# FFN inputs of twelve tiles: transposed by VectorE in 32x32 blocks and a copy through DRAM, in place of TensorE; centring moved to ScalarE

## The chip, the cores and the metric

The kernel runs on one core of a Trainium2 chip. The metric is the device time of one execution in microseconds (us). Three runs of the kernel before took 278.52, 279.04 and 279.18 us; their median is 279.04 us. One further execution was taken by the hardware profiler; every line of a profile shown here is from such an execution.

## The reference, cut to what matters

There are 2048 tokens of 512 features, in float32. Two gated residual steps follow each other:

```python
h = layernorm(x)                         # (x - mean) / sqrt(var + 1e-5), over the features
e = expert of the token's id             # 4 experts, each with one 512x512 matrix C[e]
y = (silu(h @ C[e].T) * (h @ C[e].T)) @ C[e]      # gate, up and down are the same matrix
x = x + tanh(g_xattn) * y
h = layernorm(x)
gates, which = top 2 of softmax(h @ wr.T)         # 8 routes
s = silu(silu(h @ w1.T) @ w3.T) @ w2.T
out = zeros; out[which[:, k]] += gates[:, k] * s  # the 8 rows named by the route's number, over all tokens
x = x + tanh(g_ffn) * out
```

The second step adds only to the first 8 rows of the result, so it is a weighted sum over all tokens; but each token goes through the two 512x512 layers and the routing first.

## The kernel before, in words

Tokens are sorted by expert and cut into 17 tiles ("passes") of 128. Passes 0 to 12 hold one expert each; passes 13 to 16 are mixed: four groups of 32 tokens, each with an expert of its own, so that four expert matrices are loaded for such a pass and its matmuls are 32 columns wide. The passes run in the order 0, 1, 2, 3, 4, 5, 13, 6, 7, 8, 14, 9, 10, 15, 11, 12, 16 (`order`, line 383).

A pass goes through these steps. GpSimd gathers its rows of x (`gather`, line 389). VectorE takes the mean and variance and subtracts the mean (`centre`, lines 340 to 401). TensorE transposes the tile, four 128x128 transposes into one PSUM tile tp_a, and ScalarE copies it to SBUF as hT (`turn_in`, lines 380 and 410). TensorE makes z (`up`, line 453); ScalarE and VectorE make g from it (lines 466 and 467). TensorE transposes g, ScalarE copies it as gT (`turn_mid`, line 473). TensorE makes y (`down`, line 453); VectorE adds it to x (line 481), GpSimd scatters x to the output (line 482). VectorE normalizes the new x (`norms`, lines 340 to 373 and 505), together with the inverse root for a later pass. At last TensorE transposes that (tp_f) and ScalarE copies it into hT2 (`turn_out`, line 515; lines 520 to 527 for the mixed passes, whose groups of 32 go to places known only at run time).

Every engine works through its own instructions in the order in which the code writes them; nothing is rescheduled. The loop (line 876) is a software pipeline. Iteration i issues z of the i-th pass in the order, the input transposes of the next, the centring of the one after, the gather and the matrix load of the third after, y of the pass before, tp_f of the one before that, the norm of the pass before, and the transposes of g. Matrices are loaded in SyncE's DMA queue into seven buffers (`load`, line 443), x into five.

The FFN works on two halves of 1024 tokens, hT2[0] and hT2[1]. Passes 0 to 7 fill the first. When it is complete, `sums_of_hT` issues on TensorE the logits of the router (lg, line 699), and on VectorE four sums T of quarters of hT2 (lines 598 to 602) and the transposes of the logits (lt, line 710): the first of the sums stands ahead of the two lt. Then the first layer follows as fast matrix product of seven products p1 to p7 (X, Y, Z, line 622, with additions on VectorE, line 640), routing, the second layer (v, line 730) and the weighted sum (acc). These are a generator, `ffn`, of which `step()` issues one piece; the loop calls it twice an iteration, before and after `turn_mid`, so that the pieces lie between the passes' own matmuls. logits and X come from one pool of two PSUM buffers (`ps_x`): the first X after the logits takes the buffer of the first lg. At the end of the loop the pieces that remain are issued one after another.

In the iteration in which the first half's logits are issued the second `step()` is left out:

```python
        for b in range(NB):
            if last[b] == i - 2:
                hT_sums[b] = sums_of_hT(b)
                running.append(ffn(b))
        if last[0] != i - 2:
            step()
```

Of the kernel before, what the change touches and what calls it, by code (L numbers as in the profile page):

```python
# [19 lines left out]
P = 128  # L20
# [5 lines left out]
def tile_gated_moe_ffn(  # L26
# [59 lines left out]
    xp = ctx.enter_context(tc.tile_pool(name="xp", bufs=5))  # L86
    work = ctx.enter_context(tc.tile_pool(name="work", bufs=3))
    small = ctx.enter_context(tc.tile_pool(name="small", bufs=4))
    ps_mm = ctx.enter_context(tc.tile_pool(name="ps_mm", bufs=2, space=bass.MemoryType.PSUM))
    ps_x = ctx.enter_context(tc.tile_pool(name="ps_x", bufs=2, space=bass.MemoryType.PSUM))  # L90
    ps_y = ctx.enter_context(tc.tile_pool(name="ps_y", bufs=1, space=bass.MemoryType.PSUM))
# [213 lines left out]
    def row_tables():  # L305

        pad = ct_([P, NP], F32, "pad")
        nc.vector.tensor_scalar(pad, tok, 1.0, float(4 * NT), ALU.is_lt, ALU.mult)
        nc.vector.scalar_tensor_tensor(to_row, tok, -1.0, pad, ALU.add, ALU.add)

        pads = ct_([P, E], F32, "pads")
        nc.vector.tensor_sub(pads, size[:, 2, :], num[:, 0, :])
        behind = ct_([P, E, NU - NF], F32, "behind")
        nc.vector.tensor_tensor(
            behind,
            later[:, E : 2 * E, NF:NU],
            pads.unsqueeze(2).to_broadcast([P, E, NU - NF]),
            ALU.mult,
        )
        psum = ct_([P, NU - NF], F32, "psum")  # L320
        nc.vector.tensor_reduce(psum, behind.rearrange("p e n -> p n e"), AX.X, ALU.add)
        nc.vector.tensor_sub(psum, place0[:, NF:NU], psum)
        nc.vector.tensor_scalar(
            first, psum, float(-(NB - 1) * TB), float(TB), ALU.add, ALU.min
        )


    hT2 = [ct_([P, KC, TB + (Q if b == NB - 1 else 0)], F32, f"hT2_{b}") for b in range(NB)]
    s1 = ct_([P, KC, TB], F32, "s1")
    acc = ps_acc.tile([P, D], F32, tag="acc", name="acc")  # L330
    accT = ps_acc.tile([P, KC, NR], F32, tag="acc", name="accT")
# [10 lines left out]
        nc.vector.bn_aggr(mv, st)  # L342
        return mv

    def inverse_roots(mvs_, names):


        n = range(len(names))

        def new(tag):  # L350
            return [small.tile([P, 1], F32, tag=tag, name=f"{tag}_{name}") for name in names]

        v, r, q, w, rs = new("v"), new("r"), new("q"), new("w"), new("rs")
        for i in n:
            nc.vector.tensor_scalar_add(v[i], mvs_[i][:, 1:2], EPS)
        for i in n:
            nc.vector.tensor_scalar(
                r[i].bitcast(I32), v[i].bitcast(I32), -0.5, float(0x5F3759DF), ALU.mult, ALU.add
            )
        for i in n:  # L360
            nc.vector.scalar_tensor_tensor(q[i], r[i], v[i], r[i], ALU.mult, ALU.mult)
        for i in n:
            nc.vector.tensor_scalar(w[i], q[i], 0.375, -1.25, ALU.mult, ALU.add)
        for i in n:
            nc.vector.tensor_scalar(w[i], w[i], q[i], 1.875, ALU.mult, ALU.add)
        for i in n:
            nc.vector.tensor_mul(r[i], r[i], w[i])
        for i in n:
            nc.vector.scalar_tensor_tensor(q[i], r[i], v[i], r[i], ALU.mult, ALU.mult)
        for i in n:  # L370
            nc.vector.tensor_scalar(q[i], q[i], -0.5, 1.5, ALU.mult, ALU.add)
        for i in n:
            nc.vector.tensor_mul(rs[i], r[i], q[i])
        return rs
# [22 lines left out]
    def centre(p):  # L397

        mvs[p] = moments(xs[p], f"a{p}")
        hs[p] = work.tile([P, D], F32, tag="h", bufs=4, name=f"h_a{p}")  # L400
        nc.vector.tensor_scalar(hs[p], xs[p], mvs[p][:, 0:1], None, ALU.subtract)  # L401

    def scale(*ps):
        for p, rs in zip(ps, inverse_roots([mvs.pop(p) for p in ps], [f"a{p}" for p in ps])):
            rss[p] = rs

    def turn_in(p):
        tp = transposed(hs.pop(p), f"a{p}")
# [83 lines left out]
    def norms(p_in, p_out):  # L492


        if p_out is None:
            return
        xt = x1s.pop(p_out)
        mv = [moments(xt, f"f{p_out}")]
        names = [f"f{p_out}"]
        if p_in is not None:  # L500
            mv.append(mvs.pop(p_in))
            names.append(f"a{p_in}")
        rs = inverse_roots(mv, names)
        h = work.tile([P, D], F32, tag="h", bufs=4, name=f"h_f{p_out}")
        nc.vector.tensor_scalar(h, xt, mv[0][:, 0:1], rs[0], ALU.subtract, ALU.mult)
        hs2[p_out] = h
        if p_in is not None:
            rss[p_in] = rs[-1]

    def turn_out(p):  # L510

        tp = transposed(hs2.pop(p), f"f{p}").rearrange("p (k t) -> p k t", k=KC)
        if p < NF:
            b, t = divmod(p, TB // P)
            nc.scalar.copy(hT2[b][:, :, t * P : (t + 1) * P], tp)  # L515
            return
        for i in range(G):
            n = (p - NF) * G + i
            place = NF * P + n * Q - (NB - 1) * TB
            at = nc.values_load(  # L520
                first[0:1, n : n + 1],
                engines=[ACT],
                min_val=min(place - E * (Q - 1), TB),
                max_val=min(place, TB),
                skip_runtime_bounds_check_because="its place less at most E (Q - 1) pads, at most TB",
            )
            nc.scalar.copy(hT2[NB - 1][:, :, bass.ds(at, Q)], tp[:, :, i * Q : (i + 1) * Q])

    def route(b, lt):

# [60 lines left out]
    def sums_of_hT(b):  # L591


        lgs = [logits(b, half) for half in range(2)]
        b11, b12 = hT2[b][:, 0:2, 0:HB], hT2[b][:, 0:2, HB:TB]
        b21, b22 = hT2[b][:, 2:4, 0:HB], hT2[b][:, 2:4, HB:TB]
        ts = [ffp.tile([P, 2, HB], F32, tag=f"T{i}", name=f"T{i}_{b}") for i in range(1, 5)]
        nc.vector.tensor_sub(ts[0], b12, b11)
        lts[b] = [turned(b, half, lg) for half, lg in enumerate(lgs)]
        nc.vector.tensor_sub(ts[1], b22, ts[0])  # L600
        nc.vector.tensor_sub(ts[2], b22, b12)
        nc.vector.tensor_sub(ts[3], b21, ts[1])
        return b11, b21, b22, ts

    def first_layer(b):
# [14 lines left out]
        def product(out_ps, a, bb, c, start):  # L620
            for k in range(2):
                nc.tensor.matmul(  # L622
                    out_ps,
                    a[:, k, c * P : (c + 1) * P],
                    bb[:, k, :],
                    start=start and k == 0,
                    stop=k == 1,
                    skip_group_check=True,
                )
# [62 lines left out]
    def logits(b, half):  # L692


        lg = ps_x.tile([P, P], F32, tag="x", name=f"lg_{b}_{half}")
        for k in range(KC):
            cols = hT2[b][:, k, half * HB : (half + 1) * HB].rearrange("p (t c) -> p t c", t=TT)
            for i in range(P // Q):
                nc.tensor.matmul(  # L699
                    lg[i * Q : (i + 1) * Q, :],  # L700
                    wr[:, k, :],
                    cols[:, :, i * Q : (i + 1) * Q],
                    start=(k == 0),
                    stop=(k == KC - 1),
                )
        return lg
# [116 lines left out]

    SHORT = 1
    last = {b: max(i for i, p in enumerate(order) if min(p // (TB // P), NB - 1) == b) for b in range(NB)}
    running, hT_sums, lts, w1_sums = [], {}, {}, []

    def step():
        if running:
# [23 lines left out]
    rest = slice(order[1] + 1, NU)  # L853
    nc.gpsimd.tensor_copy(held[0:1, rest], which[0:1, rest])
    first_in(order[0])
    scale(order[0])
    centre(order[1])
    scale(order[1])
    load(order[2])
# [11 lines left out]
    turn_mid(order[1])  # L871
    norms(order[3], order[0])
    load(order[4])
    summing = sums_of_w1()
    owed = []
    for i in range(2, NP + 2):
        if i < NP:
            up(order[i])
        if i + 1 < NP:
            turn_in(order[i + 1])  # L880
        if i + 2 < NP:
            centre(order[i + 2])
        if i + 3 < NP:
            gather(order[i + 3])
            load(order[i + 3])
        if i <= NP:
            down(order[i - 1])
        turn_out(order[i - 2])
        if i <= NP:
            norms(order[i + 2] if i + 2 < NP else None, order[i - 1])  # L890
        step()
        if i > NP:
            step()
        if 5 <= i < 9:
            next(summing)
        if i == 2:
            w1 = load_w(w1T, "w1")
            wr = load_w(wrT, "wr")
        if i == 7:
            w3 = load_w(w3T, "w3")  # L900
            w2 = load_w(w2T, "w2")
        if i < NP:
            turn_mid(order[i])
        for b in range(NB):
            if last[b] == i - 2:
                hT_sums[b] = sums_of_hT(b)
                running.append(ffn(b))
        if last[0] != i - 2:
            step()
    fetched = False  # L910
    while running:
        step()
# [50 lines left out]
```

## Time and profile before

| | before |
|---|---|
| median of three runs | 279.04 us |
| the profiled execution's own time | 277.53 us |
| its span, first to last instruction | 275.8 us |
| TensorE busy | 266.6 us (97%) |
| VectorE busy | 148.7 us (54%) |
| ScalarE busy | 69.3 us (25%) |
| GpSimd busy | 39.3 us (14%) |
| moved by DMA | 42.54 MB, 154 GB/s over the span |
| granted TensorE clock | 1.00 |

The span lies inside the execution's own time; the 1.7 us between them are before the first and after the last instruction. A group of the profile reads: line, engine, operation, output and inputs, shape, number of instructions, then busy microseconds, mean nanoseconds of one, and the idle time of the engine ahead of them with what ended it. A row of a timeline reads: start, duration, engine, line, operation, and in brackets the idle time ahead of it. A chain or timeline merges neighbours of one kind and gives their number. Where a row names as releaser an instruction that had long been done, something else was waited for, often a DMA. PE is TensorE, DVE VectorE, ACT ScalarE, POOL GpSimd; SPq is SyncE's queue.

### The profile page before, as it was taken

What the parts mean: (1) busy time and instruction counts of PE and PEld (TensorE: products, weight loads), DVE (VectorE), ACT (ScalarE), POOL (GpSimd) and SP (SyncE); (2) the same over time, 40 slices, a digit from 0 to 9 for tenths busy, and PEclk for the clock granted to TensorE, in tenths of its full rate; (3) what the DMA queues carried; (4) which work ended last, traced back from release to release, by engine and by line L of the source; (5) the groups of instructions that cost most, each with busy time, mean ns of one, the idle gap of its engine ahead of it and who ended that gap; (6) DMA issues with size and microseconds to landing.
All of it is one profiled execution on the core that took longest, in us unless ns stands there. A gap on an engine that the chain in (4) does not pass through costs nothing.

```text
span 275.8 us, 3562 instructions
## 1 busy us (share of the span) xinstructions
PE 266.6 (97%) x1173; PEld 125.4 (45%) x1173; DVE 148.7 (54%) x593; ACT 69.3 (25%) x134; POOL 39.3 (14%) x63
## 2 busy tenths in 40 slices
PE   5889999999999999999999999999999999999994
PEld 2445455544355454444344444534245444344362
DVE  6677877777888769918263481516253620711000
ACT  2022232232232231223143232312113233311120
POOL 6520122221122211211110010101010000000000
PEclk9999999999999999999999999999999999999999
DMA  0697998545669996697304084001000000000000
GB/s 1 217 354 277 408 402 334 173 155 206 228 225 402 389 409 258 173 398 264 112 26 166 2 312 180 38 0 40 0 12 2 0 0 1 0 0 2 0 0 2
DMA packets 20722, 42.54 MB, mean 154 GB/s; under 512 B 2143, under 2 KB 2207, under 8 KB 20704
## 3 DMA queue, kind: packets, MB, share of 16 engines
q1 hardware_dynamic: 17952, 33.66, 34.0%
q0 software_dynamic: 2720, 8.65, 8.3%
q8 instruction: 9, 0.15, 0.2%
q14 instruction: 9, 0.07, 0.1%
q10 hardware_dynamic: 32, 0.01, 0.0%
HBM read 38.10 MB, written 4.47 MB: 154 GB/s over the span
## 4 chain that ended last, share of the span: by engine, by line
PE 94%; DVE 2%; DMA 2%; issue 1%; ACT 0%; DVEq 0%
PE z L453 22%; PE y L453 21%; PE v L730 20%; PE X L622 10%; PE Y L622 5%; PE tp_f L380 3%; PE tp_a L380 3%; PE tp_g L380 3%; PE Z L622 2%; PE acc L742 1%; PE lg L699 1%; DMA x<-in_x_dram,from_row 1%; DMA idt<-in_ids_dram 1%; PE accT L758 1%; PE o L814 0%
## 5 line engine op out<-in xcount | busy, mean ns | idle before, releaser
L453 PE MATMUL z<-m,hT 128*32 128x512 f32 (+1 forms) x232 | 61.8, 595 | 0.2 <-ACT hT L428 0.2
L453 PE MATMUL y<-m,gT 128*32 128x512 f32 (+1 forms) x232 | 61.4, 594 | 0.0
L730 PE MATMUL v<-w,s 128*128 128x512 f32 (+1 forms) x136 | 57.3, 570 | 0.0
L730 PEld LDWEIGHTS v<-w,s 128*128 128x128 f32 x136 | 25.0, 190 | 27.2 <-issue 26.7
L453 PEld LDWEIGHTS z<-m,hT 128*32 128x32 f32 (+1 forms) x232 | 22.6, 146 | 29.5 <-issue 28.1
L453 PEld LDWEIGHTS y<-m,gT 128*32 128x32 f32 (+1 forms) x232 | 22.6, 146 | 27.8 <-issue 27.8
L482 POOL DMA_INDIRECT out_dram<-x,to_row x17 | 17.2, 1011 | 84.9 <-DVE x L481 82.7
L389 POOL DMA_INDIRECT x<-in_x_dram,from_row x17 | 16.7, 984 | 77.5 <-DVE h_a L401 22.9
L467 DVE SCALAR_TENSOR_TENSOR g<-z,rs_a,g 128x512 f32<-128x512 f32 x17 | 12.7, 750 | 27.1 <-ACT g L466 27.0
L466 ACT ACTIVATE g<-z,rs_a 128x512 f32<-128x512 f32 x17 | 11.7, 687 | 51.3 <-PE z L453 51.3
L481 DVE SCALAR_TENSOR_TENSOR x<-y,tg,x 128x512 f32<-128x512 f32 x17 | 12.7, 749 | 16.9 <-PE y L453 16.8
L738 ACT ACTIVATE s<-v 128x512 f32<-128x512 f32 (+1 forms) x17 | 9.7, 572 | 41.9 <-PE v L730 41.9
L515 ACT COPY hT<-tp_f 128x512 f32<-128x512 f32 x13 | 7.6, 587 | 43.5 <-PE tp_f L380 43.5
L340 DVE BATCH_NORM_STATS2 st_a<-x 128x6 f32<-128x512 f32 x16 | 11.0, 688 | 7.5 <-DMA x<-in_x_dram,from_row 7.5
L622 PE MATMUL X<-T,S 128*128 128x512 f32 x32 | 15.0, 592 | 0.0
L380 PEld LDWEIGHTS tp_f<-ident,h_f 128*128 128x128 f32 x68 | 8.2, 141 | 10.2 <-issue 10.2
L340 DVE BATCH_NORM_STATS2 st_f<-x 128x6 f32<-128x512 f32 x17 | 11.8, 695 | 0.6
L380 PEld LDWEIGHTS tp_a<-ident,h_a 128*128 128x128 f32 x64 | 7.7, 140 | 9.4 <-issue 9.1
L640 DVE TENSOR_TENSOR s<-X,c 128x512 f32<-128x512 f32 x4 | 2.8, 692 | 16.2 <-PE X L622 16.2
L473 ACT COPY gT<-tp_g 128x512 f32<-128x512 f32 x17 | 10.0, 586 | 5.3 <-PE tp_g L380 5.3
L380 PE MATMUL tp_f<-ident,h_f 128*128 128x128 f32 x68 | 10.4, 276 | 0.0
L380 PE MATMUL tp_g<-ident,g 128*128 128x128 f32 x68 | 10.2, 273 | 0.0
(165 smaller groups left out, 271.6 us busy)
## 6 DMA issues: line engine op xcount, KB each, us to landing
m<-in_ctxT_dram SPq DMA_DIRECT2D x29, 1024.0 KB
w<-in_w1T_dram SPq DMA_DIRECT2D x1, 1024.0 KB
w<-in_w3T_dram SPq DMA_DIRECT2D x1, 1024.0 KB
w<-in_w2T_dram SPq DMA_DIRECT2D x1, 1024.0 KB
x<-in_x_dram,from_row POOLq DMA_INDIRECT x17, 6.2
out_dram<-x,to_row POOLq DMA_INDIRECT x17, 6.1
wr<-in_wrT_dram SPq DMA_DIRECT2D x1, 64.0 KB
x_first<-out_dram SPq DMA_DIRECT2D x4, 4.0 KB
```

The lines of the kernel that those rows point to most:

```text
L340: nc.vector.bn_stats(st, xt)
L380: nc.tensor.transpose(tp[:, k * P : (k + 1) * P], h[:, k * P : (k + 1) * P], ident)
L389: nc.gpsimd.indirect_dma_start(out=xt, out_offset=None, in_=x, in_offset=bass.IndirectOffsetOnAxis(ap=from_row[:, p : p + 1], axis=0),)
L453: nc.tensor.matmul(out_ps[i * n : (i + 1) * n, :], lhs[:, k * P + i * n : k * P + (i + 1) * n], m[:, k, :], start=(k == 0), stop=(k == KC ...
L466: nc.scalar.activation(g, z, AF.Silu, scale=rs)
L467: nc.vector.scalar_tensor_tensor(g, z, rs, g, ALU.mult, ALU.mult)
L473: nc.scalar.copy(gT, tp)
L481: nc.vector.scalar_tensor_tensor(xt, y, tg[:, 0:1], xt, ALU.mult, ALU.add)
L482: nc.gpsimd.indirect_dma_start(out=out, out_offset=bass.IndirectOffsetOnAxis(ap=to_row[:, p : p + 1], axis=0), in_=xt, in_offset=None, bou ...
L622: nc.tensor.matmul(out_ps, a[:, k, c * P : (c + 1) * P], bb[:, k, :], start=start and k == 0, stop=k == 1, skip_group_check=True,)
L730: nc.tensor.matmul(v, s1[:, k, c_b + t * P : c_b + (t + 1) * P], w3[:, k, c0 : c0 + n], start=(k == 0), stop=(k == KC - 1),)
L738: nc.scalar.activation(s2, v, AF.Silu)
```

## The change

For the twelve passes 0 to 11 the final transposes leave TensorE and their copies leave ScalarE. VectorE transposes the normalized tile in 32x32 blocks straight into the place of a group of four passes (`set_turned`). Within a block the transpose is then right, but each quarter of the partitions still holds its own 32 tokens of every pass; a copy puts them in place. When a group of four is complete, ScalarE's DMA queue writes it to DRAM (`put`), and one iteration later reads it back in four DMAs, one for each quarter of the partitions (`fetch`). `go_on_turning` issues one of these stages an iteration, behind the centring. The mixed passes and pass 12 keep the old way. hT2 is now four tiles, one for each 512 tokens.

The centring of the passes' inputs becomes an activation on ScalarE, which computes mean minus x; the inverse root takes the other sign to make up for it. Only the first pass is centred on VectorE as before.

The first half's logits are issued two iterations later than before, and `step()` is called in every iteration.

```diff
+    NS = NF // 4 * 4
+    hT2 = [ct_([P, G, KC, P], F32, f"hT2_{b}") for b in range(NB * 2 - 1)]
+    hT2.append(ct_([P, KC, HB + Q], F32, "hT2_last"))
...
         hs[p] = work.tile([P, D], F32, tag="h", bufs=4, name=f"h_a{p}")
-        nc.vector.tensor_scalar(hs[p], xs[p], mvs[p][:, 0:1], None, ALU.subtract)
+        nc.scalar.activation(hs[p], xs[p], AF.Identity, bias=mvs[p][:, 0:1], scale=-1.0)
...
         for i in n:
-            nc.vector.tensor_scalar(q[i], q[i], -0.5, 1.5, ALU.mult, ALU.add)
+            nc.vector.tensor_scalar(q[i], q[i], -0.5 * signs[i], 1.5 * signs[i], ALU.mult, ALU.add)
...
+    def set_turned(p):
+        b, i = divmod(p, 4)
+        place = hT2[b]
+        h = hs2.pop(p)
+        nc.vector.transpose(
+            place.rearrange("p q k (i t) -> p k q i t", i=4)[:, :, :, i, :],
+            h.rearrange("p (k q t) -> p k q t", k=KC, q=4),
+        )
+        if i == 3:
+            copy = dram.tile([P, 4, KC * P], F32, tag=f"copy{b}", name=f"copy_{b}")
+            turning.append(lambda: put(place, copy))
+
+    def put(place, copy):
+        nc.scalar.dma_start(copy, place.rearrange("p q k c -> p q (k c)"))
+        turning.append(lambda: fetch(place, copy))
+
+    def fetch(place, copy):
+        for q in range(4):
+            nc.scalar.dma_start(
+                place[q * Q : (q + 1) * Q].rearrange("f g k c -> f g (k c)"),
+                copy[:, q, :].rearrange("(g f) c -> f g c", g=4),
+            )
+
+    def go_on_turning():
+        if turning:
+            turning.pop(0)()
...
         if i + 2 < NP:
             centre(order[i + 2])
+        go_on_turning()
         if i + 3 < NP:
             gather(order[i + 3])
             load(order[i + 3])
         if i <= NP:
             down(order[i - 1])
-        turn_out(order[i - 2])
+        if order[i - 2] >= NS:
+            turn_out(order[i - 2])
         if i <= NP:
             norms(order[i + 2] if i + 2 < NP else None, order[i - 1])
+            if order[i - 1] < NS:
+                set_turned(order[i - 1])
         step()
...
         for b in range(NB):
-            if last[b] == i - 2:
+            if last[b] + 2 + 2 * (b == 0) == i:
                 hT_sums[b] = sums_of_hT(b)
                 running.append(ffn(b))
-        if last[0] != i - 2:
-            step()
+        step()
```

## The prediction

> **What bounds the kernel now.** I read the page's busy shares first (TensorE 97%, VectorE 54%, ScalarE 25%), then the chain that ended last. From 15.4 us to 271 us that chain is TensorE alone: what leaves TensorE shortens the span, what makes it wait lengthens it. The chain in order of time, where the first half of the FFN starts (start, us, what):
>
> ```profile
> 101.51 0.44 PE tp_f L380 x4
> 101.94 0.44 PE tp_g L380 x4
> 102.38 1.88 PE lg L699 x64
> 104.26 3.63 PE z L453 x8
> 107.89 0.44 PE tp_a L380 x4
> 108.33 3.57 PE y L453 x32
> 111.90 0.59 PE tp_f L380 x4
> 112.49 1.72 PE X L622 x4
> ```
>
> The four transposes of a tile cost 0.44 us; after 32-column matmuls the next group costs 0.15 more, whichever it is. Between the logits lg and the first product X lie 8.2 us of other work. Then the groups, for the durations and for who waits:
>
> ```profile
> L340 DVE BATCH_NORM_STATS2 st_a<-x 128x6 f32<-128x512 f32 x16 | 11.0, 688 | 7.5 <-DMA x<-in_x_dram,from_row 7.5
> L401 DVE TENSOR_SCALAR h_a<-x,mv_a 128x512 f32<-128x512 f32 x16 | 7.8, 486 | 0.6
> L598 DVE TENSOR_TENSOR T<-hT 128x1024 f32<-128x1024 f32 x2 | 2.4, 1220 | 5.3 <-ACT hT L527 5.3
> L710 DVE STREAM_TRANSPOSE lt<-lg 128x128 f32<-128x128 f32 x4 | 1.1, 303 | 2.2 <-PE lg L699 2.2
> ```
>
> VectorE already waits for gathered x tiles, 7.5 us in all. GpSimd's timeline shows why:
>
> ```profile
> 94.17 0.98 POOL L389 DMA_INDIRECT x<-in_x_dram,from_row  x1 [6.14 <-DVE h_a L401]
> 95.45 1.02 POOL L482 DMA_INDIRECT out_dram<-x,to_row  x1 [0.30 <-DVE v_a L355]
> 102.40 0.98 POOL L389 DMA_INDIRECT x<-in_x_dram,from_row  x1 [5.93 <-DVE h_a L401]
> 103.69 1.02 POOL L482 DMA_INDIRECT out_dram<-x,to_row  x1 [0.30 <-DVE v_f L355]
> 110.91 0.98 POOL L389 DMA_INDIRECT x<-in_x_dram,from_row  x1 [6.21 <-DVE T L602]
> ```
>
> Each scatter follows its gather after 1.3 us; the next gather starts 7 us after the scatter. The VectorE instructions named had ended before, so it is the scatter's landing, whose buffer the gather takes over. The loop paces itself: nine rounds from 35.69 to 110.91, 8.36 us each. A TensorE iteration is z 3.44 + y 3.44 + three transposes of 0.44 = 8.2 us: the two are level today.
>
> **What the Trainium skill says.** "VectorE: DVE Perf Modes", The three transpose paths: VectorE transposes in 32x32 blocks only; 311 ns for 128x128, and this trace has 303. "DMA: Bandwidth & Descriptors", Anatomy of one DMA: a DMA's semaphore wait happens on the issuing sequencer, before dispatch. No dependent DMA on ScalarE's queue shows this here. "SBUF — State Buffer", Door 1 (the port swizzle): 32 partitions reach 8 of 16 ports, 189 GB/s measured against 328 for 128. No run here shows it yet. "TensorE: Matmul & The Clock Gate", Part 1: after an idle window of some 3.4 us TensorE runs at half clock until about 3.4 us of work. The trace agrees in kind: the first ten warming matmuls (line 200), after an idle start, took 3.84 us, the next 21 took 4.70, so ten cost 1.6 us too much.
>
> **The change, part by part.**
>
> Removed from TensorE: twelve tiles x 0.44 = **-5.3 us**. Removed from ScalarE: twelve copies of 0.59 (line 515), off the path.
>
> Added to VectorE: twelve block transposes of 128x512. No row has that shape. The nearest, the statistics, also pass 512 elements: 0.69 us. Not below 0.53 (T's 1.22 us for 1024 columns less the 0.69 of line 640's additions for 512: the columns without the start-up), not above four of 303 ns, 1.2 us; I take 0.69. They add 8.3 us and the centring's 7.8 leaves, in iterations where VectorE is busy 5.7 to 6.4 of 8 us: nothing. That cover gone, 0.2 us an iteration.
>
> Added to ScalarE: 16 centrings at 0.63 (nearest: Silu from SBUF to SBUF, line 647, 629 ns; bounds 0.5 and 0.75), and 15 DMA issues at 0.4 (SyncE's take 0.37, ScalarE's two at the end 0.5 each). ScalarE is three quarters idle. But in its queue gT's copy now stands behind the centring, which waits for a gather, and behind the DMAs, which wait for each other. y needs gT 3.9 us after tp_g (z and tp_a lie between): later than that, TensorE waits. The sign moved into the constants costs nothing, the instructions are the same.
>
> DMA: three tiles of 1.05 MB written and read back, 6.3 MB on 42.5. The first pair falls at 58 to 70 us, where the DMA share is 0.52 to 0.58: nothing. The second falls where it is 1.04 and more, 86 to 104 us, and beside the loads after 107. The third has about 30 us from z of the last pass to its logits and needs some 20: nothing. SyncE's queue keeps its order; lane counts of its semaphores now include ScalarE's DMAs, but those it waits for are landed long before.
>
> Moved: the first half's logits go from iteration 10 to iteration 12, and the guard that kept an FFN step from following them is gone. X now stands directly behind lg. X takes the PSUM buffer of lg's first half, so it waits for VectorE's transpose of it (line 710), which stands behind T (line 598), which stands behind the whole norm of that iteration. Before, 8.2 us covered this.
>
> Where is TensorE then, if nothing makes it wait? y(14), of a mixed pass, ended at 111.90; it has eight tp_f (3.5) and lg (1.88) less ahead of it: 106.5. Then tp_g 0.59, z 3.43, tp_a 0.44, y(9) 3.44: 114.4; tp_f(14), tp_g 0.44 each, lg 1.88: X at **117.2**.
>
> When may X start? The gather for that iteration was issued at 110.91. The loop doesn't shorten with TensorE; two small waits for VectorE in it (0.4 us) vanish, longer scatters beside 2 MB more traffic (8.0 to 8.1 us are seen in full stretches, against 6.8) give that back. Awaited gathers landed 5.9 to 7.1 us after issue; 6.9 beside the new copy: 117.8. VectorE then runs statistics 0.69 + 0.18, x 0.75, norm 3.42 (44.24 to 47.66 in its timeline), block transpose 0.69, T 1.22, lt 0.30: **125.1**. The wait is **+7.9 us**. Some of it may fall earlier, before y(9): x of pass 15 lands at 102.40 + 6.7 = 109.1, ScalarE's centring ends at 110.6, four DMA issues at 112.3, gT at 112.9, where y(9) wants it at 111.0. That 1.9 is inside the 7.9, since VectorE is later still.
>
> T also needs the copy back. Out: issued after pass 10's centring, about 102.4; 1.05 MB at half of 405 GB/s (SyncE's loads share) 5.2 us and 2 to land (the first small DMA took 1.74): 109.6. Back: issues end at 112.3; 5.2 us at half rate, up to 10.4 if 8 ports halve it again (estimate from the skill's ports), and 2: landed 118.5 to 123.5, X at 120.0 to 125.0. Just inside, at its upper end level with VectorE.
>
> Two iterations later p3 follows p5's addition in the same PSUM tile with only p4 and tp_g (3.9 us) after y; VectorE needs 0.2 + 0.75 + 3.42 + 0.69 = 5.1: **+1.2**. Before, z and y lay between.
>
> An idle stretch of 6 to 7 us would bring the slow clock back once: **+1.6**, by the first ten matmuls; bounds 0 and 3.4.
>
> Sum: -5.3 + 7.9 + 1.2 + 1.6 = **+5.4 us**. The profiled execution, 277.53 us (span 275.8, 1.7 around it), becomes 282.9; the median shown, 279.04, lies 1.5 above it: **284.4 us**.
>
> **Rivals.** *All is hidden* (0.05): X doesn't wait, -5.3, 273.7. For it: ScalarE and DMA have room on average. Against: lt behind T behind the norm is the program's order. *The gather loop follows TensorE* (0.10), the case on the other side: if scatters land sooner when VectorE and TensorE run ahead, x lies ready and VectorE starts with y(9)'s end at 114.4: 0.05 + 0.75 + 3.42 + 0.69 + 1.22 + 0.30 gives X at 120.8, +3.6 + 1.2 - 5.3 = -0.5, the clock staying: 278.5. It decides from x landing before 113.6; at 117.8 it is lost. Against: the nine even rounds. *The copy back or its traffic is the bound* (0.07): with 8 ports and a full queue it lands 4 to 9 us later than said, or holds up an expert's load: 288 to 293. For it: DMA shares of 1.04 and more; against: the tightest load, four matrices for pass 14, starts with y(13)'s end, 76.5 before and 74.3 now; 4.2 MB at 400 GB/s and 2 us to land make 87, and z(14) asks for them at 90.9 (93.91 less seven tp_f). The likeliest, 0.78, spans 280.5 to 288 by its unknowns (gather 5.9 to 7.1, clock 0 to 3.4, copy).
>
> **How the numbers follow.** Range 280.0 to 289.5: it leaves out most of the first two rivals and the top of the third. 0.3%, 0.84 us, is about what a measurement of this kernel can tell from no change. Faster 0.08 (the first rival and the edge of the second), same 0.06, slower 0.86.
>
> **What would show it.** TensorE: 12 fewer tp_f groups; 4 to 9 us idle between y(9) and the first X, ended by VectorE's lt or by the copy back; about 1 us before an X two iterations on. GpSimd's rounds still near 8.3 us. ScalarE's centring waits for gathers. The block transpose near 0.69 us. Slower matmuls right after the idle stretch, or none. I am wrong if X waits under 4 us, if gathers come at TensorE's pace, or if loads (m) end TensorE's waits.

## The result, and the profile after

The changed kernel takes **289.03 us** (median of four runs, 288.53 to 290.15) against 278.78 us before (four runs, 278.43 to 279.18): ratio **1.0373, 95% interval 1.0338 to 1.0408**. That is 10.25 us slower. The prediction was 284.4, range 280.0 to 289.5: the direction is right and the time lies inside the range, near its upper end, but the loss is nearly twice the 5.4 us that were summed. The profiled execution took 288.89 us, its span 287.2, which is 11.4 more than the span before.

TensorE's busy share is 92% (97% before). The waits of TensorE in the changed kernel (who waited, for whom: us in total, times, longest):

```profile
PE lg L745 <- DMA hT<-copy: 6.4, 1, 6.4
PE y L464 <- ACT gT L484: 3.1, 3, 1.3
...
PE tp_a L392 <- ACT hT_last L571: 1.5, 1, 1.5
PE X L668 <- DVE s L686: 0.9, 1, 0.9
...
PE tp_a L392 <- ACT h_a L413: 0.7, 1, 0.7
...
PE z L464 <- DMA m<-in_ctxT_dram: 0.2, 1, 0.2
```

None of these existed before. The largest stands between the two halves of the logits, and not in front of X. TensorE's timeline around it:

```profile
116.01 3.70 PE L464 MATMUL y<-m,gT 128*128 128x512 f32 x8 [1.31 <-ACT gT L484]
...
120.51 1.08 PE L745 MATMUL lg<-hT,wr 128*32 128x128 f32 x32
127.99 1.94 PE L745 MATMUL lg<-hT,wr 128*32 128x128 f32 x32 [6.40 <-DMA hT<-copy]
129.85 3.28 PE L668 MATMUL X<-hT,w 128*128 128x512 f32 x4
132.97 1.88 PE L668 MATMUL Z<-hT,w 128*128 128x512 f32 x4
```

The second half of lg takes 1.94 us where the first takes 1.08, and X takes 3.28 where Z, the same work, takes 1.88: after the idle stretch TensorE is slow for some 5 us (its granted clock reads 0.50 from 126 to 132 us), and by the chain below (X 3.21 us, 1.72 before; lg 1.94, half of 1.88 before) it loses 1.5 + 1.0 = 2.5 us. The chain that ended last, in order of time, names what was late:

```profile
103.94 8.36 DMA x<-in_x_dram,from_row
...
113.27 0.02 ACT h_a L413
...
113.33 0.31 ACTq L544
...
114.76 13.10 DMA hT<-copy
...
127.99 1.94 PE lg L745 x32
```

The copy back was issued behind the centring (h_a), which waited for a gather that took 8.4 us; then it needed 13.1 us to land. But VectorE's timeline shows a second chain that ended almost at the same moment:

```profile
121.71 0.69 DVE L352 BATCH_NORM_STATS2 st_a<-x 128x6 f32<-128x512 f32 x1 [3.72 <-DMA x<-in_x_dram,from_row]
...
126.74 0.71 DVE L530 STREAM_TRANSPOSE hT<-h_f 128x512 f32<-128x512 f32 x1
127.98 1.23 DVE L644 TENSOR_TENSOR T<-hT,hT 128x1024 f32<-128x1024 f32 x1 [0.53 <-DMA hT<-copy]
129.12 0.31 DVE L756 STREAM_TRANSPOSE lt<-lg 128x128 f32<-128x128 f32 x1
```

T waited 0.53 us for the copy; without it T would have begun at 127.45. So the trace alone can't say whether the copy or VectorE's late gathers set the time. The groups that answer to those shown of before:

```profile
L413 ACT ACTIVATE h_a<-x,mv_a 128x512 f32<-128x512 f32 x16 | 11.5, 722 | 54.0 <-DVE mv_a L354 54.0
L352 DVE BATCH_NORM_STATS2 st_a<-x 128x6 f32<-128x512 f32 x16 | 11.0, 690 | 22.3 <-DMA x<-in_x_dram,from_row 22.3
...
L530 DVE STREAM_TRANSPOSE hT<-h_f 128x512 f32<-128x512 f32 x12 | 8.5, 712 | 0.4
```

VectorE waits 22.3 us for gathered x, three times the 7.5 us before. GpSimd's gathers come at 35.85, 43.92, 51.84, 58.57, 69.66, 79.35, 87.76, 95.68, 103.94 and 113.75 us: nine rounds of 8.66 us (8.36 before), and the longest, 58.57 to 69.66, is the one in which the first tile is copied out. The gather of 58.57 landed 9.7 us after its issue and the scatter behind it 9.0 us, where those of the kernel before, from 35 to 105 us, took 5.4 to 7.1 and 5.2 to 7.3. The next gather, which takes over a scatter's buffer, waited for that (GpSimd's timeline; the VectorE instruction named had ended before):

```profile
69.66 0.98 POOL L401 DMA_INDIRECT x<-in_x_dram,from_row  x1 [8.79 <-DVE mv_a L354]
```

In ScalarE's queue the centring waits 54 us in all for the statistics of gathered tiles (29.6 us in the run below with the centring alone, where that cost nothing), and gT's copy stands behind the centring: TensorE's 3.1 us.

The account of the span: -5.3 (twelve tp_f) + 12.8 (the waits shown) + 2.5 (slow matmuls) = +10.0 of +11.4. The start is 0.7 us shorter in its waits, so some 2 us are assigned to nothing. They are not further waits: TensorE's idle time grew by 12.4 us (from 9.2 to 21.6), which the waits shown cover.

### The profile page after: what moved, and what is told of

Read it like the earlier page. It is cut to its first block, busy times and chain, and to the rows that moved or that the text cites. A ratio compares the mean times of both kernels' runs of the same rounds, so it can differ in the third digit from the quotient of the medians.

```text
span 287.2 us, 3489 instructions
## 1 busy us (share of the span) xinstructions
PE 265.6 (92%) x1125; PEld 121.2 (42%) x1125; DVE 148.1 (52%) x589; ACT 73.6 (26%) x138; POOL 39.7 (14%) x63
## 4 chain that ended last, share of the span: by engine, by line
PE 50%; DMA 8%; DVE 4%; issue 3%; ACTq 0%; ACT 0%; POOLq 0%; DVEq 0%
PE v L776 17%; PE X L668 10%; PE y L464 6%; PE z L464 5%; DMA hT<-copy 5%; PE Y L668 4%; DMA x<-in_x_dram,from_row 3%; PE Z L668 2%; PE acc L788 1%; PE lg L745 1%; PE accT L804 1%; DVE x L492 1%; PE tp_f L392 1%; PE tp_a L392 1%; DVE st_f L352 0%
## 5 line engine op out<-in xcount | busy, mean ns | idle before, releaser
L413 ACT ACTIVATE h_a<-x,mv_a 128x512 f32<-128x512 f32 x16 | 11.5, 722 | 54.0 <-DVE mv_a L354 54.0
L352 DVE BATCH_NORM_STATS2 st_a<-x 128x6 f32<-128x512 f32 x16 | 11.0, 690 | 22.3 <-DMA x<-in_x_dram,from_row 22.3
L392 PE MATMUL tp_a<-ident,h_a 128*128 128x128 f32 x64 | 10.0, 279 | 2.2 <-ACT hT_last L571 1.5
L392 PEld LDWEIGHTS tp_g<-ident,g 128*128 128x128 f32 x68 | 8.3, 141 | 8.5 <-issue 8.5
L693 ACT ACTIVATE s<-s 128x512 f32<-128x512 f32 x12 | 7.5, 627 | 11.0 <-DVE s L686 11.0
```

Source lines behind the costliest of these rows:

```text
L352: nc.vector.bn_stats(st, xt)
L392: nc.tensor.transpose(tp[:, k * P : (k + 1) * P], h[:, k * P : (k + 1) * P], ident)
L413: nc.scalar.activation(hs[p], xs[p], AF.Identity, bias=mvs[p][:, 0:1], scale=-1.0)
```

## The experiments

The runs below come from chips on which the kernel before takes 277.24 to 277.78 us, so ratios are compared; 1.0373 would be 287.5 to 288.1 us there (the changed kernel itself was not run on them). Four theories stood at the start. A: the copy back, late and slow, sets the time. B: VectorE's in-order chain (x, norm, block transpose, T, lt) is level with it and would set it alone. C: the gather loop, in which each gather waits for the landing of the scatter whose x buffer it takes over, is slowed by the copy's traffic and makes everything behind it late. D: the slow matmuls after the idle stretch cost time of their own.

**No copy.**

```diff
         if i == 3:
-            turning.append(lambda: put(place, copy))
+            pass
```

> The changed kernel without the copy through DRAM: put and fetch are left out, so the FFN of the first twelve passes reads tiles whose 32-row blocks are not in place. Theory A (the copy back and its traffic set the time: TensorE's 6.4 us in front of the logits' second half, the gT waits of 3.1 us behind slower gathers, the half clock of 2.5 us after it): all three go, 276 to 279 us, X waits under 1 us. Theory B (the chain of VectorE, x landing, statistics, norm, block transpose, T, lt, was level and would set it alone): lg waits for nothing, but X waits 5 to 8 us for lt instead, the half clock stays, 283 to 286 us. Rounds of the gather loop: 8.66 us under a theory in which the loop is slow by itself, 8.1 to 8.4 if the copy's traffic had slowed it.

Measured: 282.84 us against 277.35, ratio 1.0209 (1.0191 to 1.0226). So the copy costs some 4.6 us (0.0164 of the time before) and 5.5 us of loss remain without it. TensorE's waits for gT fall from 3.1 to 0.6 us; nine rounds of gathers take 8.01 us each, and the one that took 11.1 us with the copy takes 8.3: the traffic had slowed the loop, and free of it the loop comes near TensorE's pace. The wait does not vanish, it moves to X, and is smaller than B said (TensorE's waits, without the copy):

```profile
PE X L668 <- DVE lt L756: 3.6, 1, 3.6
...
PE z L464 <- DMA m<-in_ctxT_dram: 0.8, 1, 0.8
```

Both A and B hold in part. The five runs point to D, by chance: the profiled one kept its clock (0.999, and X behind the wait takes 1.98 us) and took 280.2 us, the other four had 0.983 to 0.993 and took 282.8 to 283.3. If the wait was the same in those four, of which there is no trace, the slow clock makes 2.6 to 3.1 us.

**The guard put back.**

```diff
-        step()
+        if last[0] + 4 != i:
+            step()
```

> The changed kernel with the guard of before put back: no FFN step behind the logits in their iteration, so z, tp_a and y (7.3 us) lie between lg and X. Under A nothing of the wait in front of lg's second half goes (6.4 us stay), the half clock falls on z instead, and the time is 288 to 290 us. Under B (X would have to wait for VectorE anyway, and the wait only shows itself at lg because lg comes first) the same is measured, but the wait at lg should then not fall; if the time falls by over 2 us, to below 287, the missing guard cost time by itself.

Measured: 286.04 us, ratio 1.0334 (1.0303 to 1.0365). The wait at lg stays (6.6 us). Of the two signs named, the time is below 287 us, but it did not fall by over 2 us. The interval overlaps that of the changed kernel, so the gain is not settled; the missing guard is at most a small part.

**Logits one iteration later.**

```diff
-            if last[b] + 2 + 2 * (b == 0) == i:
+            if last[b] + 2 + 3 * (b == 0) == i:
```

(lt with four buffers, h with three.)

> The changed kernel with the first half's logits, T and FFN one iteration later (lt gets four buffers and h three, to make this possible and to fit). Under A the copy back, landed at 127.9, is 2 to 6 us ahead of the logits at some 124 to 130 us: lg waits for nothing, the half clock is gone, gT's waits of 3.1 us stay (the same traffic): 280 to 283 us. Under B the wait moves with them: X waits 4 to 8 us for lt, behind the norm of that iteration, whose gather is also late: 285 to 289 us.

Measured: 294.84 us, ratio 1.0623 (1.0599 to 1.0646): slower than either theory said. lg no longer waits, but z of pass 15, which then comes ahead of the logits, waits 5.7 us for its matrices (the last at 127.6 us, just when the copy back had landed in the changed kernel), and X still waits 4.0 us for lt an iteration later. Two things follow. The stretch from 109 to 128 us is full: DMA share 0.98 at 316 GB/s in the changed kernel and 0.95 at 315 in this run, where before it was 0.74 at 262. Four matrices, the copy back and the gathers all want it, and TensorE waits for whichever it needs first. And VectorE's chain was late in both places in which the logits stood straight ahead of X.

**Six buffers for x.**

```diff
-    xp = ctx.enter_context(tc.tile_pool(name="xp", bufs=5))
+    xp = ctx.enter_context(tc.tile_pool(name="xp", bufs=6))
```

(h with three buffers, for the room.)

> The changed kernel with six buffers for x in place of five (h gets three in place of four, for the room). The gather of a pass then takes over the buffer of a scatter that is an iteration older. Theory C (the gather loop, each gather waiting for the scatter's landing, makes VectorE and through it ScalarE's gT copies, X and p3 late): gathers are issued up to 7 us earlier, VectorE's 22.3 us of waits for x fall below 8, the gT waits (3.1 us) and p3's (0.9 us) go, the copy back is issued earlier by 2 to 4 us: 280 to 284 us. If C is wrong (the copy alone is late): 287 to 289 us.

Measured: 282.4 us, ratio 1.0184 (1.0155 to 1.0214). C holds: with the copy in place, one more x buffer wins about what leaving the copy out wins (1.0184 and 1.0209). The gather now follows 0.3 us behind each scatter, VectorE's longest waits are no longer for x, gT's wait is 0.6 us, and the copy back is issued at 106.8 in place of 113.3 us; lg waits for nothing. What h's third buffer does was not run by itself. What remains is X behind lt, 3.7 us, and 1.4 us for m. TensorE's timeline from the first X on:

```profile
122.60 3.17 PE L668 MATMUL X<-hT,w 128*128 128x512 f32 x4 [3.67 <-DVE lt L756]
125.56 2.44 PE L668 MATMUL Z<-hT,w 128*128 128x512 f32 x4
127.93 2.35 PE L464 MATMUL z<-m,hT 128*32 128x512 f32 x20
```

**Six buffers and the wait filled.**

```diff
         lgs = [logits(b, half) for half in range(2)]
+        if b == 0:
+            fill = ps_y.tile([P, HB], F32, tag="y", name="fill")
+            for _ in range(8):
+                nc.tensor.matmul(fill, w1[:, 0, 0:P], w1[:, 1, :], start=True, stop=True)
```

> Six x buffers (282.4 us, X waits 3.7 us, clock 0.983 to 0.994) with eight more matmuls of 0.43 us behind the first half's logits, whose result nothing reads: they fill the 3.7 us in which TensorE would wait for lt. If the half clock after the idle stretch costs time (D), it goes with the stretch: clock 0.997 or more and 279.5 to 281 us. If X's wait alone matters and the clock not, the time stays at 282 to 283 us.

Measured: 283.3 us, ratio 1.0227 (1.0172 to 1.0282). The time doesn't show what was asked, because the filling was mis-sized: eight of these matmuls are sixteen in the profile and last 7.1 us, and X starts 3.3 us later than with the gap. But the stretch behind it answers D:

```profile
118.97 7.13 PE L642 MATMUL fill<-w 128*128 128x512 f32 x16
125.94 1.88 PE L672 MATMUL X<-hT,w 128*128 128x512 f32 x4
127.66 1.88 PE L672 MATMUL Z<-hT,w 128*128 128x512 f32 x4
129.47 1.92 PE L464 MATMUL z<-m,hT 128*32 128x512 f32 x16
```

From X to z are 3.53 us here and 5.33 us after the gap: the slow clock costs **1.8 us** after an idle stretch of 3.7 us. The run clocks are 0.992 to 0.999 with the filling, 0.983 to 0.994 without.

**Centring alone, on the kernel before.**

```diff
-        nc.vector.tensor_scalar(hs[p], xs[p], mvs[p][:, 0:1], None, ALU.subtract)
+        nc.scalar.activation(hs[p], xs[p], AF.Identity, bias=mvs[p][:, 0:1], scale=-1.0)
```

(with the signs in the constants, as in the change.)

> The kernel before with one part of the change alone: the centring as an activation on ScalarE, the sign in the constants. Theory: ScalarE's part costs nothing by itself, 277.35 plus or minus 0.8 us, y waits under 0.6 us for gT. Rival: ScalarE's in-order queue (gT's copy behind a centring that waits for the gather) delays TensorE even without the copy through DRAM: y waits 1 to 3 us for gT, 278.5 to 281 us.

Measured: 277.55 against 277.24 us, ratio 1.0005 (0.9996 to 1.0015), no wait of y for gT. By itself this part of the change costs and gains nothing.

**The changed kernel with the centring back on VectorE.**

```diff
-        nc.scalar.activation(hs[p], xs[p], AF.Identity, bias=mvs[p][:, 0:1], scale=-1.0)
+        nc.vector.tensor_scalar(hs[p], xs[p], mvs[p][:, 0:1], None, ALU.subtract)
```

> The changed kernel with the centring back on VectorE; the block transposes and the copy through DRAM stay. If the gT waits (3.1 us), tp_a's (0.7 us) and a late issue of the copy come from ScalarE's queue behind the centring, they go: 2.5 to 5 us less than the changed kernel, which on this chip is near 287.6 us (ratio 1.037 of 277.35). Rival: ScalarE's queue only passes on what the gathers and the traffic decide: within 1 us of 287.6, or above it, because VectorE carries 0.49 us more each iteration in front of its norm.

Measured: 286.22 us, ratio 1.0306 (1.0267 to 1.0345); against 1.0373 some 1.9 us less, with intervals that overlap by a little. Its trace decides between A and B better than its time. ScalarE no longer stands behind the gathers: gT's wait is 0.7 us, the copy back is issued at 105.6 us, and lg waits for nothing and ends at 117.9. Yet:

```profile
126.51 3.78 PE L668 MATMUL X<-hT,w 128*128 128x512 f32 x4 [8.61 <-DVE lt L756]
130.09 2.47 PE L668 MATMUL Z<-hT,w 128*128 128x512 f32 x4
```

VectorE waits 4.6 us for x until 118.85, then needs 7.8 us to the end of lt at 126.65. The idle stretch is no shorter than that of the changed kernel (8.6 us against 6.4), and another engine ends it: B.

**The copy's stages at the end of an iteration.**

```diff
-        go_on_turning()
         if i + 3 < NP:
...
         if i < NP:
             turn_mid(order[i])
+        go_on_turning()
```

> The changed kernel with the stage of the copy issued at the end of an iteration, behind gT's copy, in place of behind the centring: each stage comes 5 to 8 us earlier and no longer behind a gather. If only the late issue made the copy back late (A), it lands near 113 to 118 us in place of 127.9, lg waits for nothing, X waits under 4 us: 281 to 284 us (the changed kernel is near 287.5 on this chip). If VectorE's chain behind the late gather is level with it (B), the wait moves to X, 5 to 9 us for lt, as with the centring on VectorE (8.6 us, 286.2): 284.5 to 287.5 us.

Measured: 285.48 us against 277.78, ratio 1.0270 (1.0247 to 1.0293), some 2.9 us less than the changed kernel. The copy back is in time, gT waits 0.6 us, and X waits 5.8 us for lt behind a gather for which VectorE waited until 117.86: B again.

**The copy turned round: 128 partitions on the way back.**

```diff
-        nc.scalar.dma_start(copy, place.rearrange("p q k c -> p q (k c)"))
+        for q in range(4):
+            nc.scalar.dma_start(
+                copy[q * Q : (q + 1) * Q].rearrange("f g c -> g f c"),
+                place[:, q].rearrange("p k c -> p (k c)"),
+            )
...
-        for q in range(4):
-            nc.scalar.dma_start(
-                place[q * Q : (q + 1) * Q].rearrange("f g k c -> f g (k c)"),
-                copy[:, q, :].rearrange("(g f) c -> f g c", g=4),
-            )
+        nc.scalar.dma_start(place.rearrange("p g k c -> p g (k c)"), copy)
```

> The changed kernel with the copy turned round: out in four DMAs that write quarters of DRAM from 128 partitions, back in one DMA that writes all 128 partitions at once, in place of four that write 32 each. Theory of ports[...]: the copy back lands 5 to 8 us after its issue in place of 13.1, lg waits under 1 us, X 3 to 6 us for lt, 283 to 286 us. Rival, the traffic: loads, gather and copy fill the DMA engines from 109 to 128 us whatever the partitions: it lands near 127 us still, lg waits 5 to 7 us, 286.5 to 289 us.

Measured: 306.38 us, ratio 1.1044 (1.0981 to 1.1108): far slower, for a reason that neither theory named. In the chain the way out of the second tile lands 20.6 us after its issue (110.08 to 130.63), and the DMA back waits for it on ScalarE's own queue, with gT's copy behind it. ScalarE's timeline in the first such place:

```profile
78.47 0.59 ACT L484 COPY gT<-tp_g 128x512 f32<-128x512 f32 x1 [9.12 <-DMA copy<-hT]
```

y waits 17.9 us for gT in all. This agrees with the Trainium skill, "DMA: Bandwidth & Descriptors", Anatomy of one DMA: the wait of a DMA is held on the sequencer that issues it. The issue costs time as well: its four DMAs hold ScalarE's queue for 6.5 us the first time (59.15 to 65.67), where the single one of the changed kernel takes 0.4.

The third copy, where the DMA engines have little else to do, tells the two directions apart. The way out in four DMAs moves 0.10 MB per us here and takes a quarter of the engines' time (share 0.26, 204 to 207 us); the single DMA of the changed kernel moves 0.39 (186 to 188 us). The way back in one DMA to 128 partitions moves 0.43 here (217 to 218 us); in four DMAs to 32 partitions it moves 0.19 to 0.27 in the changed kernel (197 to 201 us), with the engines as busy. So the change's way back is about half as fast as this one. The size of its packets doesn't explain it, since SyncE's loads, with packets of 2 KB too, move 0.40; whether it is the ports or the order of the reads in DRAM is not shown.

**Six buffers and the guard.** Both edits shown above.

> Six buffers for x (h three) and the guard of before, both at once. If the waits are independent (X behind lt 3.7 us, half clock 1 to 2.5 us, p3 behind VectorE 0.9 us; all three lose their cause when z, tp_a and y lie between lg and X), 282.4 us of six buffers alone becomes 275.5 to 278 us, beside 277.35 before on the same chip. Rival, the loads are next: without the 3.7 us idle in front of X, z of the mixed pass 15 asks for its four matrices some 8 us earlier (about 119 instead of 127.9 us), and TensorE waits there instead; then 279 to 283 us, with m as the releaser of 3 us or more.

Measured: 283.24 us, ratio 1.0211 (1.0182 to 1.0240): the rival's case. X's wait is gone and the loads' has come. TensorE's timeline, after the first four matmuls of z at 118.60:

```profile
121.45 1.05 PE L464 MATMUL z<-m,hT 128*32 128x512 f32 x2 [1.83 <-DMA m<-in_ctxT_dram]
125.05 6.22 PE L464 MATMUL z<-m,hT 128*32 128x512 f32 x26 [2.54 <-DMA m<-in_ctxT_dram]
```

z of pass 15 now asks for its matrices at 118.6 us and has the last at 125; with X's wait ahead of it, it had asked at 127.9. SyncE issues these loads only when y of pass 14 has ended (it waits for y until 108.1 us), which frees their buffers. In the kernel before, 23 us lay between the end of that y and this z (111.8 to 134.8), with FFN pieces among them; with the logits two iterations later 10.5 us are left. The last 26 of its matmuls take 6.2 us, where all 32 of such a z take 3.6 in the trace of the filled version: the slow clock came along too (granted 0.50 from 124 to 130 us, behind a last wait of 2.5 us).

**Six buffers, guard, early copy, and the loads of w3 and w2 six iterations later.**

```diff
-        if i == 7:
+        if i == 13:
             w3 = load_w(w3T, "w3")
             w2 = load_w(w2T, "w2")
```

> Aimed at a version that beats both: six x buffers, the guard, the copy's stages at the end of an iteration, and the loads of w3 and w2 moved from iteration 7 to 13. The copy back then lies ahead of the loads for pass 15, and the loads of 74 to 100 us have 2 MB less with them. If the 5.7 us of waits for m with six buffers and guard are the two MB of w and the copy in the same stretches, they fall below 1.5 us, TensorE keeps its clock, and the time is 275.5 to 277.5 us against 277.3 before. Rival: the loads of pass 15 (4 MB in 10 us at 400 GB/s) are late by themselves once TensorE is ahead: m waits 3 us or more, 278.5 to 282 us.

Measured: 280.93 us (278.18 to 281.89) against 277.78, ratio 1.0102 (1.0062 to 1.0143). Half-way: m's waits fall from 5.7 to 3.2 us, but the 2.5 us in front of pass 15's last matrices stay: the rival's time. That the loads are late by themselves is not shown, though. SyncE issues them from 107.4 us, when y of pass 14 has ended, and from 107 to 111 us the copy back, issued by 103.2, still takes 60% of the DMA engines' time and SyncE's loads 18%.

**Logits between tp_a and y.** As the last, without the guard; the place is what is new:

```diff
+        if last[0] + 4 == i:
+            hT_sums[0] = sums_of_hT(0)
+            running.append(ffn(0))
         if i <= NP:
             down(order[i - 1])
...
-            if last[b] + 2 + 2 * (b == 0) == i:
+            if b > 0 and last[b] + 2 == i:
```

> As the version with six x buffers, guard, early copy and late w (280.93 us, before 277.78), but the first half's logits and T stand between tp_a and y of their iteration, and the guard is gone: VectorE has y's 3.4 us for T and lt, X follows y, and two steps of the FFN (7 us) lie ahead of z of pass 15, which then asks for its matrices near 125 in place of 118 us. If the loads of pass 15 (landed 123 to 125 us) and the half clock behind them were what remained, 3.2 us of waits for m and 1 to 1.8 us of half clock go: 275.5 to 277 us, faster than before by 0.3 to 0.8%. Rival: VectorE, with 5 us of T in front of the norm, becomes late for tp_a or X (2 us or more of waits for lt or h_a), 278 to 281 us.

Measured: **274.67 us** (median of six; five of them 273.85 to 274.76) against 277.73, ratio **0.9882 (0.9863 to 0.9902)**: 1.2% faster than the kernel before, and a little better than was expected. The ratio is that of the five; the sixth execution was slower than before, at 278.6 us. y covers VectorE's T and lt, and 7 us of FFN steps cover the loads of pass 15. The profiled execution is that sixth one. In its trace X waits for nothing and z for no matrix, but lg waits 2.5 us for the copy back and the y behind it takes 5.1 us in place of 3.6: together the 4.0 us by which it is longer.

```profile
115.27 1.33 PE L745 MATMUL lg<-hT,wr 128*32 128x128 f32 x32 [2.52 <-DMA hT<-copy]
116.53 5.09 PE L464 MATMUL y<-m,gT 128*128 128x512 f32 x8
```

That the other five escaped this wait follows only from their times and clocks (0.995 to 0.999).

## Why the prediction was right, and where it was not

**Removed work, -5.3.** Twelve tp_f groups are gone, as said. That the gain is real is best seen in the last experiment, which keeps 3.1 us of it: the kernel before has no wait in its loop that the other edits could have removed.

**Durations.** The block transpose takes 0.71 us (0.69 said), the centring 0.72 (0.63 said, within the bounds). The centring is free as argued: alone it changed the time by 0.0005. The block transpose was not run by itself; its 0.71 us stand in VectorE's chain to lt, where the working had put them.

**X's wait, +7.9.** The size came close (6.4 us) and the place and the releaser did not. The working said that the copy lands "just inside" and VectorE ends the wait; only its list of signs allowed for either. By the words "I am wrong if X waits under 4 us" it was wrong: the first X waited for nothing, since lg's second half had waited. The copy was last, by 0.5 us. Its way back was issued until 115.3 us (112.3 said) and landed at 127.86, 4.4 us after the upper end of what was said: the event of the third rival, which had 0.07 and whose 288 to 293 us hold the measured time. From 113.3 to 116 us its queue moved nothing, while SyncE's loads moved 1.09 MB at a full DMA share; then the two shared the engines until 127. But the experiments with centring on VectorE and with early stages show that an earlier copy only hands the same stretch to lt (8.6 and 5.8 us). The two chains were level, and that was in the working: 7.3 us from x's landing to lt were said, 7.7 are in the trace, 0.5 of them the wait for the copy. That the time still fell into the range, 0.5 us from its end, is owed to the width of the range and not to the sum.

**The step that failed** is the one that put the other waits inside the 7.9 us: "That 1.9 is inside the 7.9, since VectorE is later still", and with it "the first pair falls at 58 to 70 us ... nothing". (The share there, 0.52 to 0.58 in the working, is 0.42 on the mean in the trace of before, and 0.95 from 62 to 66 us; with the copy it is 0.83.) A stall ahead of the logits isn't inside a later wait when the later wait hangs on the same loop. The first copy stretched a round of the gather loop to 11.1 us. y of pass 13 waited 1.2 us for gT behind it, and three more waits (1.5 for hT_last, 0.7 and 1.3 around y(9)) followed before the logits. TensorE reached lg at 120.5 us, where the working has 115.3 (X at 117.2 less 1.9), and the gather of that iteration was issued at 113.75, not 110.91, and landed 8.0 us later, not 6.9. Both moved back together, so the wait at the end kept its size and the earlier ones came on top. The working judged the DMA by its share of time, and not by the latency of the one transfer in the loop that paces everything. Six buffers, which take that latency out of the loop, and leaving out the copy, which shortens it, each gave back about 5 us.

**p3, +1.2:** 0.9 us, near what was said. **Slow clock, +1.6 (0 to 3.4):** it came, 2.5 us in the changed kernel, 1.8 measured by itself. The page of the Trainium skill that was used, "TensorE: Matmul & The Clock Gate", Part 1, with an idle window of some 3.4 us, fits in kind, but that figure is no threshold here. The granted clock fell to 0.50 behind waits of 2.5 us in three traces (six buffers with the guard, where 1.8 us of waiting came shortly before; the version with w later; the last version), and stayed at 1.00 behind one of 3.6 us in the trace without the copy.

**SyncE's lanes** were said to be landed long before. They were not: in the changed kernel SyncE waits 7.9 us for a copy back and 1.4 us for a copy out to land before it issues matrices. TensorE's only wait for m, 0.2 us, lies at the start (19.3 us), so it was harmless here.

**The rival on the other side,** that gathers follow TensorE, had X wait 3.6 us. Where the loop is freed (no copy; six buffers) X waits 3.6 and 3.7 us. Its mechanism and figure are right under those conditions; its total, 0.5 us less than before, was not. It assumed full clock and no waits for m; but also the one execution without the copy that kept its clock took 2.9 us more than before, of which 1.4 us are waits for m and gT and some 2 us are assigned to nothing.

## What to carry to other kernels

Before counting what leaves the bounding engine as gain, list what feeds it at each place where it will now be earlier (here the gathers, the copy, VectorE's chain, the expert loads); when these are level, removing one wait shows the next, and the gain comes only when each has other work as its cover. A loop of gather and scatter through a fixed number of buffers turns added DMA latency into longer rounds, whatever the mean share of the DMA engines says; one more buffer was worth as much here as the whole copy. Waits ahead of a later wait add to it when both hang on that loop.

## What the runs showed of the hardware

- TensorE's granted clock fell to 0.50 behind idle stretches of 2.5 us (three traces), 2.9 us (the copy turned round) and 3.7 to 8.6 us, and not behind one of 3.6 us (no copy) and one of 3.0 us (the copy turned round, where y at 79.10 takes 3.64 us). It came back after 3 to 6 us of work. The matmuls behind cost 1.5 us more after 2.5 us (y in the last version), 1.8 after 3.7 us and about 2.5 after 6.4 us. After 8.6 us X and Z took 3.78 and 2.47 us in place of 1.88 each.
- Gathers of 128 rows that shared the DMA with a copy and the loads landed after 9.7 and 8.4 us beside a way out and 7.2 and 8.0 us beside a way back; in the kernel before, beside the loads alone, those from 35 to 105 us landed after 5.4 to 7.1.
- With the DMA engines to itself, a copy of 1.05 MB from DRAM moved 0.43 MB per us as one DMA to 128 partitions and 0.19 to 0.27 as four DMAs to 32 partitions each; to DRAM 0.39 as one DMA and 0.10 as four that each write a quarter of it.
- Eight float32 matmuls of 128x128 by 128x512 stood as sixteen in the profile and took 7.1 us.
